# Two row tiles' attention logits on the two row halves of TensorE, with the keys held twice and W1 and W2 multiplied on chip

## The chip, the cores and the metric

The kernel runs on one core of a Trainium2 chip. A core has a matrix engine (TensorE, PE in the profile; its weight loads are listed apart as PEld), VectorE (DVE), ScalarE (ACT), GpSimd (POOL) and SyncE (SP, which here only issues transfers). Each engine works through its own instruction queue in order, and engines wait for each other through semaphores. TensorE writes its results to PSUM; ACT or DVE carry them on to SBUF. The metric is the device time of one execution in microseconds (us), the median over runs.

## The reference

A graph of 3327 nodes with 256 features goes through two layers; a dense weighted adjacency matrix `adj` is given. All values are float32. What matters for the change is the attention of layer 0, which is computed twice:

```
h  = relu(layernorm(x))                     # (3327, 256)
Xf = Xa = h
for n in range(2):
    q = Xa @ W1.T @ W2.T                    # (3327, 64)
    k = Xa @ W3.T                           # (3327, 64)
    probs = softmax(q @ k.T)                # (3327, 3327)
    A  = the largest probs of each row that reach 0.9 of its sum, renormalized
    Xf = R @ Xf                             # R: adj + identity, rows normalized
    Xa = A @ Xa
    Z  = Z + Xf @ U1[n].T + Xa @ U2[n].T
x = x + layernorm(h + Z) * ln_g + ln_b
```

Layer 1 is a graph attention with four heads over `adj > 0`; the change does not touch it.

## The kernel before

Rows are cut into 26 tiles of 128 (`NT`, the last one partly padding), and the tiles are worked on in 13 groups of two. A fast path (`fast`) runs first, and a slow general path only if a check at the end asks for it. In the profiled execution all the work shown is that of the fast path.

**Start.** The 26 tiles of x are loaded by SP's queue, DVE takes row statistics, DVE and ACT apply LayerNorm and relu (L553 to L555). Meanwhile ACT's queue issues the loads of W1, W3, W2, U1 and U2 (L545 to L549).

**Each of the two steps** has a prologue over all 26 tiles (L798 to L809). It transposes a tile on PE (`transposed`, L563, copied by ACT at L565), multiplies by W3 to get the transposed keys `kt`, 64 partitions by 3328 columns (L571, copied at L802), multiplies again to get the keys untransposed (L805, copied by ACT into `kk` at L808), and accumulates their second moments and their sum (L809), which go to `gm` (L810).

Then come the groups. `exponentials` takes the two tiles of a group one after the other. For each it makes the query in a chain of PE and ACT steps: transpose (L563, L565), times W1 (L571, L585), times W2 (L587, L589), and times `gm`, which yields the mean and the second moment of the row's logits (L591, copied at L593, finished by DVE at L594 and L595). Then it computes the tile's logits in seven chunks of 512 keys, each one matmul over 64 partitions (L604) into a PSUM buffer `pl`, from which ACT takes the exponential into `e` (L605), with row sums into `parts`. DVE adds the sums up (L608). A float32 matmul shows as two MATMUL records in the profile.

`top_p` finds each row's threshold on DVE. It begins with a Gaussian guess made of the mean and second moment: ACT needs its Ln table for L630 and its Exp table for L631, and again Ln at L633 and Exp at L645 and L648, each change of table being a load. It then evaluates masked sums over the 3327 exponentials (L660, two tiles per evaluation, four evaluations in step 0 and five in step 1), takes candidates (L703 to L728) and clears what falls below the threshold (L730).

`full_step` computes R @ Xf for a tile: SP loads the tile's columns of the transposed adjacency (L739), PE accumulates 26 matmuls (L741), DVE adds the tile itself (L743) and ACT divides (L746). `attention_step` computes A @ Xa: PE transposes `e` in blocks of four (L757) into a PSUM buffer `pt`, ACT copies them (L759), PE multiplies them (L766); each block's transposes are issued ahead of the previous block's matmuls. In step 1, `add_up` transposes the four results (L785, also into `pt`), multiplies by U1 and U2 into `z` (L791, a buffer of the pool `ps_m`), and DVE adds it to `main` (L792).

**Order.** The loop (L813 to L832) asks for the exponentials of the next group, then the full steps, `top_p` and attention of the present one. The program text does not fix the order on an engine: a planner orders each engine's instructions from the text, the dependences and the free buffers, so that L741 for instance is placed between the links of the query chain. The order is then fixed, and each queue works in it.

**Buffers.** PSUM tiles come from four pools of two buffers each: `ps_l` (logits, `pl`), `ps_acc` (accumulators), `ps_t` (`pt`) and `ps_m` (`pm`: all the small results of the chains, and `z`). `epool` holds four tiles of exponentials, two groups' worth.

Of the kernel before, what the change touches and what calls it, by code (L numbers as in the profile page):

```python
# [9 lines left out]
F32 = mybir.dt.float32  # L10
# [3 lines left out]
AF = mybir.ActivationFunctionType  # L14
ALU = mybir.AluOpType
# [453 lines left out]
def fast(  # L469
# [33 lines left out]
    def ln_stats(pool, t):  # L503
        st = pool.tile([P, V.BN_STATS_DIM], F32, name="bst")
        V.bn_stats(st, main[:, t, :D])
        V.bn_aggr(mv[:, t, :], st)
# [8 lines left out]
    with ExitStack() as l0:  # L515
        wpool = l0.enter_context(tc.tile_pool(name="wpool", bufs=1))
        w1 = wpool.tile([P, 2, DA], F32, name="w1")
        w3 = wpool.tile([P, 2, DA], F32, name="w3")
        w2 = wpool.tile([DA, DA], F32, name="w2")
        u1 = wpool.tile([P, STEPS, 2, D], F32, name="u1")  # L520
# [4 lines left out]
        xa1 = wpool.tile([P, NT, D + 1], F32, name="xa1")  # L525
        kt = wpool.tile([DA, NP], F32, name="kt")
        gm = wpool.tile([DA, 2 * DA + 1], F32, name="gm")
        V.tensor_copy(gm[:, :DA], ident[:DA, :DA])

# [7 lines left out]
        ps_acc = l0.enter_context(tc.tile_pool(name="ps_acc", bufs=2, space=PSUM))  # L537
        ps_t = l0.enter_context(tc.tile_pool(name="ps_t", bufs=2, space=PSUM))
        ps_m = l0.enter_context(tc.tile_pool(name="ps_m", bufs=2, space=PSUM))


        for t in range(NT):
            nc.sync.dma_start(main[:, t, :D], x[t * P : (t + 1) * P, :])
            ln_stats(small, t)
        nc.scalar.dma_start(w1, w1t.rearrange("(c p) o -> p c o", p=P))  # L545
        nc.scalar.dma_start(w3, w3t.rearrange("(c p) o -> p c o", p=P))
        nc.scalar.dma_start(w2, w2t)
        nc.scalar.dma_start(u1, u1t.rearrange("n (c p) o -> p n c o", p=P))
        nc.scalar.dma_start(u2, u2t.rearrange("n (c p) o -> p n c o", p=P))  # L549
# [18 lines left out]
        def projected(w, xt):  # L568
            ps = ps_m.tile([DA, P], F32, name="pm")
            for c in range(2):  # L570
                T.matmul(ps, w[:, c, :], xt[:, c, :], start=(c == 0), stop=(c == 1))  # L571
            return ps

        def exponentials(src, tiles):


            G = len(tiles)
            sm = small.tile([P, G], F32, name="sm")
            mu = small.tile([P, G], F32, name="mu")
            sq = small.tile([P, G], F32, name="sq")  # L580
            es = []
            for g, t in enumerate(tiles):
                ps = projected(w1, transposed(src, t))
                ut = small.tile([DA, P], F32, name="ut")
                S.copy(ut, ps)  # L585
                ps = ps_m.tile([DA, P], F32, name="pm")
                T.matmul(ps, w2, ut, start=True, stop=True)  # L587
                qt = small.tile([DA, P], F32, name="qt")
                S.copy(qt, ps)  # L589
                ps = ps_m.tile([P, 2 * DA + 1], F32, name="pm")  # L590
                T.matmul(ps, qt, gm, start=True, stop=True)  # L591
                qg = small.tile([P, 2 * DA + 1], F32, name="qg")
                S.copy(qg, ps)  # L593
                V.tensor_copy(mu[:, g : g + 1], qg[:, 2 * DA :])  # L594
                V.scalar_tensor_tensor(  # L595
                    qg[:, :DA], qg[:, :DA], 1.0, qg[:, DA : 2 * DA], ALU.mult, ALU.mult, accum_out=sq[:, g : g + 1]
                )
                e = epool.tile([P, NP], F32, name="e")
                nc.gpsimd.memset(e[:, N:], 0.0)
                parts = small.tile([P, NC], F32, name="parts")  # L600
                for c in range(NC):
                    w = min(512, N - 512 * c)
                    pl = ps_l.tile([P, 512], F32, name="pl")
                    T.matmul(pl[:, :w], qt, kt[:, 512 * c : 512 * c + w], start=True, stop=True)  # L604
                    S.activation(  # L605
                        e[:, 512 * c : 512 * c + w], pl[:, :w], AF.Exp, accum_out=parts[:, c : c + 1]
                    )
                V.tensor_reduce(sm[:, g : g + 1], parts, AX.X, ALU.add)  # L608
                es.append(e)
            return es, sm, mu, sq  # L610

# [183 lines left out]
        for n in range(STEPS):  # L795
            srcf, srca = (main, main) if n == 0 else (xf1, xa1)
            acc = ps_acc.tile([P, D + 1], F32, name="acc")
            for t in range(NT):  # L798
# [5 lines left out]
                for c in range(2):  # L804
                    T.matmul(ps, xt[:, c, :], w3[:, c, :], start=(c == 0), stop=(c == 1))  # L805
                kk = small.tile([P, DA + 1], F32, name="kk")
                nc.gpsimd.memset(kk[:, DA:], 1.0)
                S.copy(kk[:, :DA], ps)  # L808
                T.matmul(acc[:DA, : DA + 1], kk[:p, :DA], kk[:p, :], start=(t == 0), stop=(t == NT - 1))  # L809
            S.activation(gm[:, DA:], acc[:DA, : DA + 1], AF.Copy, scale=1.0 / N)  # L810
            groups = [list(range(t, min(t + 2, NT))) for t in range(0, NT, 2)]
# [240 lines left out]
```

## Time and profile before

| | |
|---|---|
| Median of 3 runs | 3086.12 us (3082.74 to 3088.73) |
| Profiled execution, its own time | 3073.39 us |
| Its span, first to last instruction | 3071.6 us |
| PE busy | 2756.5 us (90%) |
| DVE busy | 2387.5 us (78%) |
| ACT busy | 835.3 us (27%) |
| Mean granted PE clock | 0.923 |
| L604, logits on PE | 407.1 us in 728 records |
| L741, R @ Xf on PE | 336.4 + 335.8 us |
| L766, A @ Xa on PE | 322.8 + 323.3 us |

A group of lines names the line, engine and operation, what is written and read, how often, and the busy time. In a timeline, each row has the start, the length, the engine, the line, and in brackets how long the engine had sat idle before it and what ended that wait. Two clocks matter for PE: "PEclk" or "clock" is the share of its full speed that it was granted. A busy PE is not a PE at its peak, since matmuls are pipelined and their ends are modelled.

### The profile page before, as it was taken

Reading aid. Unit: us, or ns where it says so; the run is one execution under the profiler, and the core shown is the slowest. Engines: PE = TensorE matmul, PEld = TensorE weight load, DVE = VectorE, ACT = ScalarE, POOL = GpSimd, SP = SyncE. Lnnn points to the kernel's source line nnn. Section 1 sums busy time; section 2 is a strip of 40 time slices with the busy share of each in tenths; the row PEclk is TensorE's granted clock in tenths of the full one; section 3 lists DMA queues with packets and bytes.
Section 4 is the critical chain, followed back from the end, with each engine's and each line's share of the span. In section 5 each row is a group of like instructions: output and inputs, shape, how many; then the busy total and the mean of one; then the engine's idle time right before and its main releaser. Section 6 shows DMA issues by size and latency. Waiting matters only on the chain.

```text
span 3071.6 us, 32112 instructions
## 1 busy us (share of the span) xinstructions
PE 2756.5 (90%) x11078; PEld 1781.1 (58%) x11078; DVE 2387.5 (78%) x6069; ACT 835.3 (27%) x2036; POOL 54.5 (2%) x167
## 2 busy tenths in 40 slices
PE   6949999999999999389999999999995599999997
PEld 4427676666667685167777667666685433333334
DVE  3189887878788820899988888888893799999997
ACT  2423333333333324233233333333321300000000
POOL 0000000000000000000000000000001100000000
PEclk9759899999999999599999999999998799999998
DMA  3001111111111111001111111100121132222211
GB/s 108 23 0 45 45 45 45 45 45 45 45 45 45 45 56 34 0 11 41 49 48 47 48 47 49 49 31 33 38 71 37 52 104 83 82 77 71 89 55 33
DMA packets 77213, 150.69 MB, mean 49 GB/s; under 512 B 5489, under 2 KB 63600, under 8 KB 77040
## 3 DMA queue, kind: packets, MB, share of 16 engines
q1 hardware_dynamic: 74656, 146.56, 14.7%
q10 hardware_dynamic: 2384, 1.98, 0.2%
q8 instruction: 89, 1.46, 0.2%
q14 instruction: 84, 0.69, 0.1%
HBM read 145.11 MB, written 3.41 MB: 48 GB/s over the span
## 4 chain that ended last, share of the span: by engine, by line
PE 57%; DVE 33%; ACT 6%; issue 3%; DMA 1%; POOL 0%; ACTq 0%; DVEq 0%; POOLq 0%; SPq 0%
PE acc L950 19%; DVE y L660 18%; PE acc L741 13%; PE pl L604 11%; DVE cands L703 4%; PE acc L766 4%; PE pm L791 2%; PE pm L571 2%; ACT e L605 1%; PE pt L757 1%; ACT L630 1%; PE pm L805 1%; ACT L631 1%; PE pm L563 1%; DVE e L730 1%
## 5 line engine op out<-in xcount | busy, mean ns | idle before, releaser
L950 PE MATMUL acc<-e,hp 128*65 128x512 f32 (+1 forms) x1456 | 585.6, 562 | 1.8 <-DVE e L947 1.8
L947 DVE SCALAR_TENSOR_TENSOR e<-both,low,mask 128x512 f32<-128x512 f32 (+1 forms) x728 | 469.2, 708 | 38.4 <-PE acc L950 38.4
L660 DVE SCALAR_TENSOR_TENSOR y<-e,nt 128x3327 f32<-128x3327 f32 x130 | 478.8, 3683 | 2.3
L604 PE MATMUL pl<-kt,qt 64*128 64x512 f32 (+1 forms) x728 | 407.1, 698 | 54.8 <-ACT e L605 54.8
L950 PEld LDWEIGHTS acc<-e,hp 128*65 128x65 f32 x1456 | 198.1, 138 | 368.4 <-issue 255.3
L759 ACT COPY et<-pt 128x512 f32<-128x512 f32 (+1 forms) x364 | 199.4, 555 | 744.6 <-PE pt L757 744.6
L741 PE MATMUL acc<-main,at 128*128 128x257 f32 x1352 | 336.4, 402 | 0.1
L741 PE MATMUL acc<-xf,at 128*128 128x257 f32 x1352 | 335.8, 397 | 0.3 <-ACT xa L770 0.3
L766 PE MATMUL acc<-xa,et 128*128 128x257 f32 x1352 | 322.8, 382 | 3.8 <-ACT et L759 3.8
L766 PE MATMUL acc<-main,et 128*128 128x257 f32 x1352 | 323.3, 383 | 0.2
L604 PEld LDWEIGHTS pl<-kt,qt 64*128 64x128 f32 x728 | 144.2, 222 | 291.8 <-ACT e L605 229.4
L741 PEld LDWEIGHTS acc<-main,at 128*128 128x128 f32 x1352 | 262.6, 200 | 52.0 <-issue 13.3
L757 PE MATMUL pt<-ident,e 128*128 128x128 f32 x1352 | 202.1, 274 | 94.0 <-DVE e L730 94.0
L741 PEld LDWEIGHTS acc<-xf,at 128*128 128x128 f32 x1352 | 256.5, 197 | 49.4 <-issue 14.0
L766 PEld LDWEIGHTS acc<-xa,et 128*128 128x128 f32 x1352 | 245.4, 191 | 36.8 <-ACT et L759 7.6
L766 PEld LDWEIGHTS acc<-main,et 128*128 128x128 f32 x1352 | 245.0, 190 | 35.6 <-ACT et L759 6.2
L605 ACT ACTIVATE e<-pl 128x512 f32<-128x512 f32 (+1 forms) x364 | 205.2, 564 | 154.2 <-PE pl L604 151.2
L757 PEld LDWEIGHTS pt<-ident,e 128*128 128x128 f32 x1352 | 168.6, 141 | 127.7 <-DVE e L730 95.1
L703 DVE MAX8 cands<-y 128x8 f32<-128x208 f32 x832 | 237.2, 360 | 0.5
L660 DVE SCALAR_TENSOR_TENSOR y<-e,up 128x3327 f32<-128x3327 f32 x52 | 191.6, 3684 | 1.8
L730 DVE SCALAR_TENSOR_TENSOR e<-e,met 128x3327 f32<-128x3327 f32 x52 | 191.4, 3680 | 0.0
L660 DVE SCALAR_TENSOR_TENSOR y<-e,t 128x3327 f32<-128x3327 f32 x52 | 191.3, 3679 | 0.0
(183 smaller groups left out, 2091.9 us busy)
## 6 DMA issues: line engine op xcount, KB each, us to landing
at<-in_adjt_dram SPq DMA_DIRECT2D x104, 832.0 KB, 4.4
adjb<-in_adjt_dram SPq DMA_DIRECT2D x78, 512.0 KB, 3.6
main<-in_x_dram SPq DMA_DIRECT2D x26, 128.0 KB, 3.2
xh<-in_x_dram SPq DMA_DIRECT2D x26, 128.0 KB, 2.0
xr<-in_x_dram SPq DMA_DIRECT2D x26, 128.0 KB, 2.1
adjb<-in_adjt_dram SPq DMA_DIRECT2D x13, 256.0 KB, 2.7
out_dram<-r SPq DMA_DIRECT2D x25, 128.0 KB, 1.8
u<-in_u1t_dram ACTq DMA_DIRECT2D x1, 512.0 KB, 5.9
```

The lines of the kernel that those rows point to most:

```text
L571: T.matmul(ps, w[:, c, :], xt[:, c, :], start=(c == 0), stop=(c == 1))
L604: T.matmul(pl[:, :w], qt, kt[:, 512 * c : 512 * c + w], start=True, stop=True)
L605: S.activation(e[:, 512 * c : 512 * c + w], pl[:, :w], AF.Exp, accum_out=parts[:, c : c + 1])
L660: V.scalar_tensor_tensor(y, e[:, :N], th[:, k : k + 1], e[:, :N], ALU.is_lt, ALU.mult, accum_out=sums[:, k : k + 1])
L703: V.max(cands[:, k, c, :], y[:, c * PIECE : min(c * PIECE + PIECE, N)])
L730: V.scalar_tensor_tensor(e[:, :N], e[:, :N], nxt, e[:, :N], ALU.is_gt, ALU.mult)
L741: T.matmul(acc, at[:, j - j0, :], src[:, j, :], start=(j == 0), stop=(j == NT - 1))
L757: T.transpose(pt[:, k, :], e[:, (j0 + k) * P : (j0 + k + 1) * P], ident)
L759: S.copy(et[:, :n, :], pt[:, :n, :])
L766: T.matmul(acc, et[:, j - j0, :], src[:, j, :], start=(j == 0), stop=(j == NT - 1))
L947: V.scalar_tensor_tensor(e[:, k, :w], both[:, k, :w], low[:, j, k : k + 1], mask[:, j % JC, :w], ALU.max, ALU.mult)
L950: T.matmul(acc[k][:, :w], hp[:, j, k, :], e[:, k, :w], start=(j == 0), stop=(j == NT - 1))
```

## The change

The two tiles of a group now share one query tile `qt`: the first tile's transposed query lies in partitions 0 to 63, the second's in 64 to 127. The keys `kt` and the moments `gm` are held twice, in both halves. For that, W3 is held twice side by side, so that one 128-column multiplication writes both copies of the keys, and the query weights likewise. W1 and W2 are multiplied once at the start to `w12` (a transpose and a matmul for each half of W1's 256 rows), so the query chain loses one link.

`exponentials` first makes both queries and their moments, and then goes through the seven chunks, issuing for each chunk one matmul per tile, from partitions 0 to 63 and from 64 to 127, into the two banks of one `pl` buffer. ACT takes the two exponentials one after the other, and DVE adds up both tiles' sums in one instruction at the end. A `pl` buffer now takes two PSUM banks, and `ps_t` and `ps_m` have one buffer instead of two. In the prologue, ACT copies the untransposed keys twice into `kk`, and `gm` is written by two instructions.

```diff
-        w1 = wpool.tile([P, 2, DA], F32, name="w1")
-        w3 = wpool.tile([P, 2, DA], F32, name="w3")
-        w2 = wpool.tile([DA, DA], F32, name="w2")
+        w12 = wpool.tile([P, 2, 2, DA], F32, name="w12")
+        w3 = wpool.tile([P, 2, 2, DA], F32, name="w3")
...
-        kt = wpool.tile([DA, NP], F32, name="kt")
-        gm = wpool.tile([DA, 2 * DA + 1], F32, name="gm")
-        V.tensor_copy(gm[:, :DA], ident[:DA, :DA])
+        kt = wpool.tile([P, NP], F32, name="kt")
+        gm = wpool.tile([P, 2 * DA + 1], F32, name="gm")
+        for o in (0, DA):
+            V.tensor_copy(gm[o : o + DA, :DA], ident[o : o + DA, o : o + DA])
...
-        ps_t = l0.enter_context(tc.tile_pool(name="ps_t", bufs=2, space=PSUM))
-        ps_m = l0.enter_context(tc.tile_pool(name="ps_m", bufs=2, space=PSUM))
+        ps_t = l0.enter_context(tc.tile_pool(name="ps_t", bufs=1, space=PSUM))
+        ps_m = l0.enter_context(tc.tile_pool(name="ps_m", bufs=1, space=PSUM))
...
+        w1 = small.tile([P, 2, DA], F32, name="w1", bufs=1)
+        w2 = small.tile([DA, DA], F32, name="w2", bufs=1)
         nc.scalar.dma_start(w1, w1t.rearrange("(c p) o -> p c o", p=P))
-        nc.scalar.dma_start(w3, w3t.rearrange("(c p) o -> p c o", p=P))
         nc.scalar.dma_start(w2, w2t)
+        for r in range(2):
+            nc.scalar.dma_start(w3[:, :, r, :], w3t.rearrange("(c p) o -> p c o", p=P))
+        for c in range(2):
+            ps = ps_m.tile([DA, P], F32, name="pm")
+            T.transpose(ps, w1[:, c, :], ident)
+            w1r = small.tile([DA, P], F32, name="w1r")
+            S.copy(w1r, ps)
+            ps = ps_m.tile([P, DA], F32, name="pm")
+            T.matmul(ps, w1r, w2, start=True, stop=True)
+            for r in range(2):
+                S.copy(w12[:, c, r, :], ps)
...
         def projected(w, xt):
-            ps = ps_m.tile([DA, P], F32, name="pm")
+            ps = ps_m.tile([P, P], F32, name="pm")
             for c in range(2):
-                T.matmul(ps, w[:, c, :], xt[:, c, :], start=(c == 0), stop=(c == 1))
+                T.matmul(
+                    ps, w[:, c].rearrange("p r o -> p (r o)"), xt[:, c, :], start=(c == 0), stop=(c == 1)
+                )
...
+            qt = small.tile([P, P], F32, name="qt")
             es = []
             for g, t in enumerate(tiles):
-                ps = projected(w1, transposed(src, t))
-                ut = small.tile([DA, P], F32, name="ut")
-                S.copy(ut, ps)
-                ps = ps_m.tile([DA, P], F32, name="pm")
-                T.matmul(ps, w2, ut, start=True, stop=True)
-                qt = small.tile([DA, P], F32, name="qt")
-                S.copy(qt, ps)
+                half = slice(g * DA, g * DA + DA)
+                ps = projected(w12, transposed(src, t))
+                S.copy(qt[half], ps[half])
                 ps = ps_m.tile([P, 2 * DA + 1], F32, name="pm")
-                T.matmul(ps, qt, gm, start=True, stop=True)
+                T.matmul(ps, qt[half], gm[half], start=True, stop=True)
...
-                parts = small.tile([P, NC], F32, name="parts")
-                for c in range(NC):
-                    w = min(512, N - 512 * c)
-                    pl = ps_l.tile([P, 512], F32, name="pl")
-                    T.matmul(pl[:, :w], qt, kt[:, 512 * c : 512 * c + w], start=True, stop=True)
-                    S.activation(
-                        e[:, 512 * c : 512 * c + w], pl[:, :w], AF.Exp, accum_out=parts[:, c : c + 1]
-                    )
-                V.tensor_reduce(sm[:, g : g + 1], parts, AX.X, ALU.add)
                 es.append(e)
+            parts = small.tile([P, G, NC], F32, name="parts")
+            for c in range(NC):
+                lo, w = 512 * c, min(512, N - 512 * c)
+                pl = ps_l.tile([P, G, 512], F32, name="pl")
+                for g in range(G):
+                    half = slice(g * DA, g * DA + DA)
+                    T.matmul(pl[:, g, :w], qt[half], kt[half, lo : lo + w], start=True, stop=True)
+                for g, e in enumerate(es):
+                    S.activation(e[:, lo : lo + w], pl[:, g, :w], AF.Exp, accum_out=parts[:, g, c : c + 1])
+            V.tensor_reduce(sm, parts, AX.X, ALU.add)
...
-                    T.matmul(ps, xt[:, c, :], w3[:, c, :], start=(c == 0), stop=(c == 1))
-                kk = small.tile([P, DA + 1], F32, name="kk")
-                nc.gpsimd.memset(kk[:, DA:], 1.0)
-                S.copy(kk[:, :DA], ps)
-                T.matmul(acc[:DA, : DA + 1], kk[:p, :DA], kk[:p, :], start=(t == 0), stop=(t == NT - 1))
-            S.activation(gm[:, DA:], acc[:DA, : DA + 1], AF.Copy, scale=1.0 / N)
+                    T.matmul(ps, xt[:, c, :], w3[:, c, 0, :], start=(c == 0), stop=(c == 1))
+                kk = small.tile([P, 2 * DA + 1], F32, name="kk")
+                nc.gpsimd.memset(kk[:, 2 * DA :], 1.0)
+                for r in range(2):
+                    S.copy(kk[:, r * DA : r * DA + DA], ps)
+                T.matmul(acc[:, : DA + 1], kk[:p, : 2 * DA], kk[:p, DA:], start=(t == 0), stop=(t == NT - 1))
+            for o in (0, DA):
+                S.activation(gm[o : o + DA, DA:], acc[o : o + DA, : DA + 1], AF.Copy, scale=1.0 / N)
```

## The prediction

> **What bounds the kernel now.** I read the page's summary first, then busy time by window, then the timeline of one group of two row tiles, PE, ACT and DVE together.
>
> ```profile
> PE 2756.5 (90%) x11078; PEld 1781.1 (58%) x11078; DVE 2387.5 (78%) x6069; ACT 835.3 (27%) x2036; POOL 54.5 (2%) x167
> ...
> PEclk9759899999999999599999999999998799999998
> ```
>
> The averages only say that PE leads and DVE follows. PE's clock is low at the start of each attention step. By window (busy us and instructions of PE, PEld, DVE, ACT, POOL, then clock, DMA share, GB/s):
>
> ```profile
> 110.00:200.00 90.00, 63.66 (x115) 26.57 (x114) 45.65 (x146) 38.87 (x101) 0.00 (x0) 0.50 0.00 0
> ...
> 200.00:397.00 197.00, 171.48 (x753) 130.33 (x754) 180.84 (x473) 56.01 (x131) 0.59 (x6) 0.89 0.11 35
> ...
> 700.99:776.35 75.36, 71.56 (x305) 52.07 (x305) 60.94 (x168) 26.22 (x62) 0.20 (x2) 0.93 0.14 46
> ...
> 1865.88:1951.25 85.37, 80.65 (x357) 59.61 (x357) 72.80 (x197) 29.05 (x67) 0.20 (x2) 0.96 0.13 44
> ```
>
> There are three regimes. At a step's start two groups of logits run at clock 0.50. Then DVE binds for about three groups (180.84 of 197), because full_step matmuls were already done in the prologue. From about the fourth group on PE binds: one group takes some 76 us in step 0 and 85.4 in step 1, with PE nearly full and DVE at 61 and 73. In the list of the longest pieces of the critical chain, L703 starts at 248.91 and 311.02, 62 us apart: the DVE-bound period of step 0. In step 1 it starts at 1286.48 and, three groups on, at 1508.67: 74 us. So a PE saving counts down to 62 and 74, not below.
>
> Inside a group, the logits of the second tile (start, length, engine, line, what, count, wait):
>
> ```profile
> 700.83 6.35 PE L604 MATMUL pl<-kt,qt 64*128 64x512 f32 x14
> ...
> 712.70 1.28 ACT L630 ACT_TABLE_LOAD   x1
> ...
> 714.21 1.28 ACT L631 ACT_TABLE_LOAD   x1
> ...
> 715.62 0.58 ACT L605 ACTIVATE e<-pl 128x512 f32<-128x512 f32 x1
> ...
> 716.18 0.59 ACT L605 ACTIVATE e<-pl 128x512 f32<-128x512 f32 x1
> ...
> 716.34 6.33 PE L604 MATMUL pl<-kt,qt 64*128 64x512 f32 x8 [2.48 <-ACT e L605]
> ...
> 722.60 21.57 PE L741 MATMUL acc<-main,at 128*128 128x257 f32 x92
> ...
> 723.22 0.16 DVE L608 TENSOR_REDUCE sm<-parts 128x1 f32<-128x7 f32 x1 [11.08 <-ACT e L605]
> ```
>
> The first tile takes 6.3 us for seven chunks of two instructions. In the second, the Ln and Exp table loads hold ACT's in-order queue, PE fills its two pl buffers, idles 2.48 us and comes back at half speed: weight loads 0.85 us apart instead of 0.43. So 14 instructions need 6.28 us in one tile and 11.73 us (710.87 to 722.60) in the other. About 1.8 us more of slow clock falls in the first L741 matmuls (92 in 21.57, against 0.215 each at full speed). DVE idles 11.08 us for these logits. ACT alone does a chunk in 0.56 us (715.62 to 716.18, both inputs ready).
>
> **What the Trainium skill says.** "TensorE: Matmul & The Clock Gate", Part 3 (The mechanism): matmuls at different row groups overlap, while starts and ends stay in program order. Before uses only rows 0 to 63, so no trace of it shows this. Its Part 1 puts an idle array at half clock and restores it after some 3.4 us of activity. The trace agrees on the half, but at 138.72 us fourteen 64-row matmuls take 11.29 us and stay at half. "TensorEngine Tiling (Array Packing)", Gotcha 1: row tiles must write different PSUM banks. The pl tile does, at two banks per buffer. "PSUM — Partial Sum Buffer", "The four PSUM rules": eight banks. Before uses 2+2+2+2, after 4+2+1+1, which is why ps_t and ps_m fall to one buffer.
>
> **The change part by part**, per group unless said otherwise.
>
> *Removed, L585/L587.* One matmul pair (0.43 us of PE) and its ACT copy. The link is 1.0 us long (709.03 to 710.02) but hidden by 0.70 us of L741. I take 0.43 x 2 = 0.9 us (0.9 to 2).
>
> *Logits as pairs of half arrays.* Same instruction count. Unknown: does fp32, which runs here as two instructions per product, overlap between halves? Bounds: a pair costs 0.86 us if yes, 1.71 if no, and 1.71 or 3.42 at half clock. I take yes. Unwaited ACT then needs 1.12 a pair. var (L628) now exists before the logits begin, so I place the two table loads after the first exponential or two, as before after the second tile's first chunk. PE then has done pairs 0 and 1 by 2.15 us, and ACT is free again near 4.7. Pair 0's second exponential frees its buffer near 5.4. PE has idled about 3 us and I take half clock again: 4.5 pairs x 1.71 = 7.7, end 13.1, with 0.5 us of latency 13.6. Before: 6.28 + 11.73 = 18.0. Gain 4.4. If the clock stays full, 9 + 3 = 12 and no residue of 1.8: gain 7.8. With 0.9 for L587: 5.3 a group, up to 8.7.
>
> *Order.* Both query chains now come before all logits. Their waits were covered by L741 (eight instructions at 707.27 to 710.87) and still can be; uncovered, the second chain costs 2.8 us.
>
> *ps_t 2 to 1.* An attention tile starts with two transpose blocks back to back:
>
> ```profile
> 1905.94 1.04 PE L757 MATMUL pt<-ident,e 128*128 128x128 f32 x8
> ...
> 1906.57 1.07 ACT L759 COPY et<-pt 128x512 f32<-128x512 f32 x2 [7.66 <-PE pt L757]
> ...
> 1907.21 2.01 PE L766 MATMUL acc<-xa,et 128*128 128x257 f32 x8 [0.24 <-ACT et L759]
> ```
>
> The second block must now wait for the first copy: 0.5 + 0.8 + 0.5 = 1.85 us instead of 1.28, so 0.55 us a tile. Later blocks are covered: a copy is over (1910.32) 0.7 us before the next transposes (1911.02). I take 0.8 a group (0 to 1.1). In step 1 add_up's second L785 also shares the buffer: 0.5 more.
>
> *ps_m 2 to 1.* z of add_up (L789) holds the only buffer until DVE's L792, and the next group's L563 waits for it:
>
> ```profile
> 1947.38 0.38 PE L563 MATMUL pm<-ident,xa 128*128 128x128 f32 x2
> ...
> 1947.80 0.40 DVE L792 SCALAR_TENSOR_TENSOR main<-xh,pm 128x256 f32<-128x256 f32 x1
> ```
>
> That is 1 us, or up to 3.7 if L792 stands behind one L660 pass. Behind L563 on PE stand the query chain and the logits. Step 1 penalty in all: 2.3 (0.8 + 0.5 + 1). In the prologue L805 must wait for the kt copy: L563's successor comes 0.65 us later per tile, 34 us over both steps uncovered. L741 can cover it as it covers the other waits there (six instructions in each 3.2 us tile). I take 10.
>
> *Rest.* The second kk copy (0.21 us on ACT) is in those 0.65. 128-column weight loads in L571: L805 already issues 128-column loads at 0.13 us each, no slower than L571's 0.15, so nothing. W1 x W2 and the second w3 DMA fall under the x loads and LayerNorm (first matmul at 24.31 us, ACT idle until 21.23); uncovered about 6 us, two 2 to 3 us landings. One L608 in place of two and two gm writes: under 0.3 us.
>
> *Step start.* Group 0's sm comes at 134.90, 26.7 us after its first logit at 108.24. After: 108.24 - 1.0 + 2.8 + 13.6 + 0.9 = 124.5, 10 us earlier, and DVE, which binds next, starts 10 us earlier. Twice: 20.
>
> **Sum.** PE-bound groups: ten a step (logits 3 to 12). Step 0: 10 x (5.3 - 0.8) = 45. Step 1: 10 x (5.3 - 2.3) = 30. Starts 20, prologues -10. Net 85 us off the profiled execution's 3073.4 (span 3071.6), 2988. The runs shown have their median 12.7 us above it, so 3001: I say 3000. Periods become 71.5 and 82.4, still above the DVE floors of 62 and 74.
>
> **Rivals.**
> 1. *More than this.* The paired halves keep or regain full clock: 10 x 7.9 + 10 x 6.4 + 10 + 10 = 163 to 173 less, about 2920. If L741 is also placed into the logits' waits, the DVE floor ends it: 10 x 14 + 10 x 11 less, about 2850. For: full-array L741 does recover the clock. Against: before never has L741 between logits.
> 2. *The halves do not overlap* (the change doesn't do what it says), and this ends slower. A pair is 3.42 us once the clock is half, and the stall now falls at the head of both tiles, not of one: 5.4 + 4.5 x 3.42 = 20.8 against 18.0. Less 0.9, plus 0.8 and 2.3: 2.7 and 4.2 a group, 69 over twenty, plus 10 for prologues: about 3160. For: no trace shows fp32 overlap. Against: halves use separate rows and banks. It decides from about 2.6 us a pair at half clock.
> 3. *The single buffers eat the gain.* Attention starts 29 us, prologues 34, and L792 twice behind an L660 pass in ten groups, 74: 137 against a gross gain of 126, about 3095. For: DVE is in order and 3.7 us passes are its bulk. Against: the waits in before are filled.
>
> **How the numbers follow.** Main case 0.50 (its own range 2955 to 3040), rival 1 0.18 (2850 to 2955), rival 2 0.20 (3100 to 3190), rival 3 0.12 (3040 to 3115). About 0.08 of rival 1 lies below 2900 and 0.10 of rival 2 above 3150: range 2900 to 3150. A change within 0.2% (6 us) can't be told from none. Faster: 0.50 + 0.18 + 0.02 of rival 3 = 0.70. Same: 0.04. Slower: 0.20 + 0.06 = 0.26.
>
> **What would show it.** Right: pairs of the new L604 0.86 us apart at full clock or 1.71 at half, ACT's exponentials two close together, one PE idle of about 3 us per group near the head of the logits, group periods near 71 and 82, first sm of a step 10 us earlier. Wrong: pairs at 3.42 (rival 2); clock at 1.0 through the logits or L741 among them (rival 1); PE waiting on L792 or on L759 for more than 2 us a group (rival 3); or L630 waiting in ACT's queue for a mu that DVE has not yet made.

## The result, and the profile after

The changed kernel takes 11800.47 us (median of four runs, 11791.0 to 11803.16) against 3084.43 us (3080.19 to 3088.73) for the kernel before, run beside it: a ratio of 3.8252, with a 95% interval of 3.8186 to 3.8319. The forecast of 3000 us, with a range of 2900 to 3150, is wrong by a factor of almost four, and no case that it weighed comes near.

The profile of the changed kernel, its summary and one row of its slices:

```profile
span 11800.7 us, 65994 instructions
...
PE 5473.1 (46%) x21848; PEld 3558.9 (30%) x21848; DVE 10757.8 (91%) x14142; ACT 2380.0 (20%) x4448; POOL 108.8 (1%) x278
...
PEclk7999899999766666666665666666666666658998
```

PE issues 21848 matmul records where it had issued 11078, DVE works 10757.8 us where it had worked 2387.5, and the span has twice the instructions. A change of PE's order or of PSUM buffers can't do that: work has been added. The costliest groups of the page, by line, say which:

```profile
L196 DVE SCALAR_TENSOR_TENSOR scr<-e,cand 128x3327 bf16<-128x3327 f32 x1404 | 5124.4, 3684 | 35.6 <-ACT e L177 12.7
...
L676 DVE SCALAR_TENSOR_TENSOR y<-e,nt 128x3327 f32<-128x3327 f32 x130 | 478.8, 3683 | 2.3
```

L676 is the masked sum of the fast path (L660 before). L196 stands in `general`, the path that runs only if the verdict at the end of `fast` asks for it: 1404 passes are 27 for each of 26 tiles in each of two steps. The timelines show where it begins. The kernel before ends its fast path with the verdict, and little follows:

```profile
3063.68 0.14 DVE L1005 TENSOR_SCALAR redo<-bad 1x1 int32<-1x1 f32 x1
```

In the changed kernel (the same statement is L1023):

```profile
3040.27 0.15 DVE L1022 TENSOR_TENSOR bad<-verdict 1x1 f32<-1x1 f32 x1
3040.45 0.14 DVE L1023 TENSOR_SCALAR redo<-bad 1x1 int32<-1x1 f32 x1
3041.32 0.84 SPq L123 DMA_DIRECT2D main<-in_x_dram  x2
```

The verdict comes 23.2 us earlier than before. Then x is loaded anew (L123), and the whole network is computed a second time, from 3041 to 11800 us. So there are two questions: why the verdict changed, and why the fast path gained 23 us where 85 were forecast.

**Where the fast path's 23 us come from.** Marks in both timelines: the start of the last write of `gm` in each step (L810, now L828), of the copy of a group's sums into `met` (L624, now L640), and of `redo`. A negative difference is a gain.

| Stretch | before, us | after, us | difference | forecast |
|---|---|---|---|---|
| start and prologue of step 0, to `gm` | 106.2 | 140.0 | +33.8 | +10 for both prologues |
| to the third group's sums | 160.0 | 146.2 | -13.9 | -10 |
| ten group periods, to the last sums of step 0 | 760.7 | 704.7 | -56.0 | -45 |
| end of step 0 and prologue of step 1, to `gm` | 174.6 | 207.9 | +33.3 | (above) |
| to the third group's sums | 181.6 | 169.0 | -12.6 | -10 |
| ten group periods, to the last sums of step 1 | 845.2 | 831.6 | -13.6 | -30 |
| the rest, to `redo` | 835.4 | 841.2 | +5.8 | 0 |
| sum, to `redo` | 3063.7 | 3040.5 | -23.2 | -85 |

**The logits.** One group of the changed kernel, step 0, on PE:

```profile
690.10 1.88 PE L622 MATMUL pl<-kt,qt 64*128 64x512 f32 x4
...
692.98 1.99 PE L622 MATMUL pl<-kt,qt 64*128 64x512 f32 x8
695.47 1.13 PE L622 MATMUL pl<-kt,qt 64*128 64x512 f32 x4 [0.51 <-ACT e L624]
699.65 2.93 PE L622 MATMUL pl<-kt,qt 64*128 64x512 f32 x8 [3.06 <-ACT e L624]
```

The eight records at 692.98 are two pairs of logits, four float32 products of 64 by 512, in 1.99 us. Within a pair the two products start 7 ns apart: the halves overlap, as forecast. The four records at 690.10 are only two products, one after the other, and they take nearly as long, 1.88 us. The planner had put the first tile's first two products (685.90 and 687.65) ahead of the second tile's query, so that in this group, as in most later ones, five of the seven pairs run side by side and two do not. The forecast had all seven side by side. PE then idles 3.06 us for ACT, as forecast. The same group on ACT:

```profile
694.74 0.59 ACT L624 ACTIVATE e<-pl 128x512 f32<-128x512 f32 x1
...
695.44 1.28 ACT L646 ACT_TABLE_LOAD   x1
...
696.95 1.28 ACT L647 ACT_TABLE_LOAD   x1
...
698.36 0.58 ACT L624 ACTIVATE e<-pl 128x512 f32<-128x512 f32 x1
```

The two table loads come after the third pair, not after the first exponential or two, so only the last two pairs follow PE's pause. They take 2.93 us, although the last chunk has only 255 columns. The same group on DVE:

```profile
691.13 3.68 DVE L746 SCALAR_TENSOR_TENSOR e<-e,met 128x3327 f32<-128x3327 f32 x1
694.73 0.15 DVE L642 TENSOR_TENSOR var<-mu 128x2 f32<-128x2 f32 x1
...
703.81 0.17 DVE L625 TENSOR_REDUCE sm<-parts 128x2 f32<-128x14 f32 x1 [8.52 <-ACT e L624]
...
705.32 0.16 DVE L650 TENSOR_TENSOR u<-u,mu 128x2 f32<-128x2 f32 x1 [0.95 <-ACT u L649]
```

DVE finishes the group before (L746), makes `var`, and has nothing to do until the sums: 8.52 us, plus 0.95 for the Ln of the guess. In the kernel before, a group had 11.08 for the sums (the line of L608 in the prediction), and:

```profile
711.37 0.15 DVE L594 COPY mu<-qg 128x1 f32<-128x1 f32 x1 [0.72 <-ACT qg L593]
...
724.73 0.16 DVE L634 TENSOR_TENSOR u<-u,mu 128x2 f32<-128x2 f32 x1 [0.96 <-ACT u L633]
```

That is 3.3 us less in a group, and the period fell by 3.5, from 75.4 to 71.9.

**The prologue.** The window of step 0's prologue (PE, PEld, DVE, ACT and POOL busy, clock, DMA share, GB/s), before and then after:

```profile
24.00:106.20 82.20, 74.86 (x419) 51.83 (x420) 9.62 (x31) 30.69 (x107) 2.46 (x25) 1.00 0.13 44
```

```profile
24.00:139.80 115.80, 89.67 (x418) 68.37 (x418) 10.26 (x33) 34.11 (x133) 2.46 (x26) 0.77 0.10 32
1124.00:1198.80 74.80, 57.61 (x255) 43.55 (x254) 0.59 (x2) 17.15 (x72) 1.57 (x16) 0.66 0.08 26
```

The same 418 or 419 matmul records take 33.6 us more. PE is idle for 26.1 us of them instead of 7.3, and busy for 14.8 us longer, since the clock falls from 1.00 to 0.77. The last row is the latter part of step 1's prologue, at 0.66. The planner fills waits of the prologue with matmuls of the full steps (L757); they are its cover. The last of them starts at 82.9 us. From there to the prologue's end the clock is 0.54, and a tile looks like this on PE:

```profile
93.20 1.12 PE L821 MATMUL pm<-w,xt 128*128 128x64 f32 x4 [0.35 <-ACT kt L818]
94.91 0.66 PE L826 MATMUL acc<-kk 128*128 128x65 f32 x2 [0.58 <-ACT kk L825]
95.36 0.63 PE L577 MATMUL pm<-ident,main 128*128 128x128 f32 x2
96.51 1.22 PE L586 MATMUL pm<-xt,w 128*128 128x128 f32 x4 [0.52 <-ACT xt L579]
98.09 1.12 PE L821 MATMUL pm<-w,xt 128*128 128x64 f32 x4 [0.35 <-ACT kt L818]
```

With one `pm` buffer each of a tile's three small results waits for ACT's copy of the one before it, and each piece runs at half clock. A tile takes 4.89 us (93.20 to 98.09). In the kernel before, the cover ends too, at 92.0 us, but with two `pm` buffers a tile then takes 1.98 us, at a clock of 1.00:

```profile
93.98 0.30 PE L809 MATMUL acc<-kk 128*64 128x65 f32 x2 [0.24 <-ACT kk L808]
94.25 0.65 PE L571 MATMUL pm<-xt,w 128*64 128x128 f32 x4
94.83 0.66 PE L805 MATMUL pm<-w,xt 128*128 128x64 f32 x4
95.33 0.39 PE L563 MATMUL pm<-ident,main 128*128 128x128 f32 x2
95.96 0.30 PE L809 MATMUL acc<-kk 128*64 128x65 f32 x2 [0.25 <-ACT kk L808]
```

With the cover between the links a tile takes 3.54 us, against 3.18 before.

### The profile page after: what moved, and what is told of

Its sections match the earlier page's. It is cut to its first block, busy times and chain, and to the rows that moved or that the text cites. A ratio compares the mean times of both kernels' runs of the same rounds, so it can differ in the third digit from the quotient of the medians.

```text
span 11800.7 us, 65994 instructions
## 1 busy us (share of the span) xinstructions
PE 5473.1 (46%) x21848; PEld 3558.9 (30%) x21848; DVE 10757.8 (91%) x14142; ACT 2380.0 (20%) x4448; POOL 108.8 (1%) x278
## 4 chain that ended last, share of the span: by engine, by line
DVE 73%; PE 19%; ACT 4%; issue 3%; DMA 1%; another core or an unknown queue 0%; POOL 0%; SPq 0%; ACTq 0%; POOLq 0%; DVEq 0%
DVE scr L196 38%; DVE y L676 6%; PE acc L968 5%; DVE e L435 3%; DVE junk L385 3%; DVE scr L214 3%; DVE e L443 3%; PE acc L255 2%; PE pl L171 2%; DVE scr L218 2%; DVE e L210 2%; DVE e L219 2%; PE acc L757 1%; PE acc L782 1%; DVE e L439 1%
## 5 line engine op out<-in xcount | busy, mean ns | idle before, releaser
L196 DVE SCALAR_TENSOR_TENSOR scr<-e,cand 128x3327 bf16<-128x3327 f32 x1404 | 5124.4, 3684 | 35.6 <-ACT e L177 12.7
L444 PE MATMUL acc<-e,hp 128*65 128x512 f32 (+1 forms) x1456 | 717.9, 641 | 347.7 <-DVE e L443 347.7
L968 PE MATMUL acc<-e,hp 128*65 128x512 f32 (+1 forms) x1456 | 585.6, 562 | 2.0 <-DVE e L965 2.0
L676 DVE SCALAR_TENSOR_TENSOR y<-e,nt 128x3327 f32<-128x3327 f32 x130 | 478.8, 3683 | 2.3
L435 DVE SCALAR_TENSOR_TENSOR e<-both,sd,e 128x512 f32<-128x512 f32 (+1 forms) x728 | 471.5, 707 | 8.9 <-ACT e L434 8.9
L434 ACT ACTIVATE e<-both,dlow 128x512 f32<-128x512 f32 (+1 forms) x728 | 443.8, 678 | 51.9 <-PE acc L444 51.9
L443 DVE SCALAR_TENSOR_TENSOR e<-adjb,e 128x512 f32<-128x512 f32 (+1 forms) x728 | 427.3, 646 | 4.6 <-ACT e L440 4.4
L440 ACT ACTIVATE e<-e 128x2048 f32<-128x2048 f32 (+1 forms) x182 | 325.4, 1788 | 245.9 <-DVE e L439 245.7
L385 DVE CUSTOM_DVE_ANT_0 junk<-an,db 128x3327 bf16<-128x3327 f32 (+1 forms) x104 | 370.7, 3624 | 2.0 <-ACT db L370 1.2
L214 DVE TENSOR_TENSOR_SCAN scr<-scr 128x3327 uint16<-128x3327 bf16 x52 | 368.5, 7086 | 0.0
L255 PE MATMUL acc<-main,et 128*128 128x257 f32 x1352 | 353.2, 409 | 0.0
L255 PE MATMUL acc<-xa,et 128*128 128x257 f32 x1352 | 343.2, 400 | 3.8 <-ACT et L248 3.8
L782 PE MATMUL acc<-xa,et 128*128 128x257 f32 x1352 | 328.5, 388 | 0.0
L782 PE MATMUL acc<-main,et 128*128 128x257 f32 x1352 | 321.8, 382 | 0.0
L757 PE MATMUL acc<-main,at 128*128 128x257 f32 x1352 | 320.2, 392 | 0.0
```

Of the source, the lines that this page charges most:

```text
L196: V.scalar_tensor_tensor(junk, e[:, :N], cand[:, g : g + 1], e[:, :N], ALU.is_ge, ALU.mult, accum_out=sums[:, g : g + 1],)
L214: V.tensor_tensor_scan(rank, ties, ties, 0.0, ALU.add, ALU.max)
L255: T.matmul(acc, et[:, j - j0, :], src[:, j, :], start=(j == 0), stop=(j == NT - 1))
L385: V.tensor_tensor_reduce(junk[:p], an[:p], db[:p, k, :N], scale=1.0, scalar=-BIG, op0=ALU.add, op1=ALU.max, accum_out=top[:p, t, k : k + 1],)
L435: V.scalar_tensor_tensor(e[:, k, :w], both[:, 0, k, :w], sd[:, j, 1, k : k + 1], e[:, k, :w], ALU.add, ALU.max)
L443: V.scalar_tensor_tensor(ek, adjb[:, :n, j % JC, :], 0.0, ek, ALU.is_gt, ALU.mult)
```

## The experiments

The theory for the second run of the network: the verdict asks for it because W1 x W2 multiplied first rounds the queries differently, which makes one row's threshold fall between two equal exponentials. The test is L1000: the number of exponentials kept, `met[:, 2]`, must equal the number strictly above the largest one dropped, `met[:, 4]`. The rivals: another condition of the verdict, or a fault of the half arrays or of the doubled keys. Ratios below are to the kernel before, run beside each experiment (about 3078 us each time).

### e1_chain: the queries through W1 and W2 again, all else of the change kept

```diff
...
-                ps = projected(w12, transposed(src, t))
+                xt = transposed(src, t)
+                ps = ps_m.tile([DA, P], F32, name="pm")
+                for c in range(2):
+                    T.matmul(ps, w1[:, c, :], xt[:, c, :], start=(c == 0), stop=(c == 1))
+                ut = small.tile([DA, P], F32, name="ut")
+                S.copy(ut, ps)
+                ps = ps_m.tile([P, P], F32, name="pm")
+                T.matmul(ps, w2.rearrange("p r o -> p (r o)"), ut, start=True, stop=True)   # w2 held twice
...
```

> The changed kernel with one part undone: queries again by W1 and then W2 (W2 held twice side by side), keys and moments still held twice, logits still side by side, one buffer each in ps_t and ps_m. Theory R (rounding): the product W1 x W2 rounds the queries otherwise, and with these numbers one row's smallest kept exponential equals a dropped one exactly, so the verdict orders the general path; with the old rounding it does not, and the time is that of the fast path, about 3063 us plus or minus 12 (the changed kernel's fast path ends 23 us earlier than before's; the chain gets its link back). Theory H (halves): something that the half arrays or the doubled keys and moments deliver trips the verdict; then the general path still runs and the time is about 11800 us.

3117.96 us, a ratio of 1.0137 (1.0103 to 1.0172), and no second run. With the old rounding and the new halves the verdict is content. It is some 55 us slower than expected; the time is taken up under e12.

### e2_w12_only: the kernel before, with W1 x W2 alone

```diff
...
-                ps = projected(w1, transposed(src, t))
-                ut = small.tile([DA, P], F32, name="ut")
-                S.copy(ut, ps)
-                ps = ps_m.tile([DA, P], F32, name="pm")
-                T.matmul(ps, w2, ut, start=True, stop=True)
+                ps = projected(w12, transposed(src, t))
```

> The kernel before with one part of the change alone: W1 and W2 multiplied once on chip, everything else as before (one tile after the other, keys held once, two buffers in all pools). Theory R: the rounding is that of the changed kernel, the general path runs, about 3080 + 8760 = 11830 us. Theory H: no general path, about 3060 to 3085 us.

11804.58 us in its one run. Its page has the second path's group again, with neither halves nor doubled keys in the kernel:

```profile
L196 DVE SCALAR_TENSOR_TENSOR scr<-e,cand 128x3327 bf16<-128x3327 f32 x1404 | 5124.2, 3683 | 32.1 <-ACT e L177 9.3
```

So the product W1 x W2 is enough for it, and the halves are not needed.

### e3_no_tie_test and e4_tie_but_one_tile: the changed kernel, the tie condition left out

```diff
         V.tensor_tensor(one, met[:, 2], met[:, 4], ALU.not_equal)
+        V.memset(one[:, 47:48], 0.0)       # e4 only: tile 21 of step 1
         V.tensor_add(bad, bad, one)        # e3: this line and the first taken out
```

> The changed kernel with one of the verdict's five conditions left out, the one that compares the number of kept exponentials with the number of those strictly above the largest dropped one (met rows 2 and 4, a tie at the cut). Theory R: no general path, about 3061 us (23 below before), plus or minus 5. Theory H, through the window's count, a full piece of candidates, the range of the sum or the logits' reach: still about 11800 us.

> The changed kernel with the tie condition kept for all row tiles of both steps except tile 21 of step 1 (column 47 of met), where it is left out. Theory R in its sharpest form, one row in that one tile: no general path, about 3061 us. If ties are spread over several tiles, or lie in another: about 11800 us.

e3: 3050.43 us, 0.9909 (0.9873 to 0.9946). e4: 3054.1 us in one run. The tie condition alone asks for the second run, and of the 52 tiles of both steps only tile 21 of step 1 raises it. A float32 calculation of the attention off the chip, which had named this tile, finds it in one row: its smallest kept exponential and its largest dropped one are the same number. The row itself is shown by no run.

### e5_after_swapped_order and e6_before_swapped_order: only the order of a sum changed

```diff
-        def projected(w, xt):
+        def projected(w, xt, order=(0, 1)):
...
-            for c in range(2):
-                T.matmul(..., start=(c == 0), stop=(c == 1))
+            for c in order:
+                T.matmul(..., start=(c == order[0]), stop=(c == order[1]))
...
-                ps = projected(w12, transposed(src, t))
+                ps = projected(w12, transposed(src, t), (1, 0))     # e6: w1
```

The query's two halves of 128 features are added up in the other order. e5 does it in the changed kernel, e6 in the kernel before; the verdict is whole in both.

> The changed kernel, whole, with its verdict whole, and one difference that costs nothing: the query's matmul adds up its two halves of 128 features in the other order (second half first), which only rounds the queries otherwise. Theory R: the tie is an accident of rounding and a float32 calculation of this order has none, so no general path: about 3050 us, as in the run without the tie test, plus or minus 8. A rival, that the product W1 x W2 or the half arrays make values that tie or go wrong whatever the order: about 11800 us.

> The kernel before, with nothing of the change, and the same swap of order in its query matmul (W1, second half of the features first). Theory R: rounding alone decides; a float32 calculation of this order has one tie, in tile 13 of step 1, so the general path runs, about 3085 + 8760 = 11845 us. Rival, that before's structure is safe from ties: about 3080 us.

e5: 3047.24 us, 0.9894 (0.9853 to 0.9935). e6: 11817.42 us in one run; the page of e6 has:

```profile
L196 DVE SCALAR_TENSOR_TENSOR scr<-e,cand 128x3327 bf16<-128x3327 f32 x1404 | 5124.3, 3684 | 35.6 <-ACT e L177 12.7
```

This settles it: the same mathematics and the same instructions, added in another order, and the changed kernel is 1.1% faster than before, or the kernel before takes 11817 us. The calculation off the chip puts e6's tie in another tile, 13 of step 1. Of four roundings of the queries (two orders, with and without the product), two ask for the second run. e5 is therefore no safer than the rest; it has a rounding without a tie for these inputs. From here on e5 is the changed kernel with its fast path alone, and the next experiments are built on it.

### e9_one_half: both queries in partitions 0 to 63

```diff
-            qt = small.tile([P, P], F32, name="qt")
+            qts = [small.tile([DA, P], F32, name="qt%d" % g) for g in range(G)]
...
-                    half = slice(g * DA, g * DA + DA)
+                    half = slice(0, DA)
+                    qt = qts[g]
```

> As the changed kernel with swapped order (3047 us), but both tiles' queries lie in partitions 0 to 63, so both logits of a pair use the same half of the array; everything else, the order of issue too, is kept. Theory O (the halves overlap, and that is what the groups won): pairs 1.71 us apart at full clock and 3.42 at half instead of 0.86 and 1.71, 6 to 8 us more a group in some twenty groups and 10 more for each of the four groups at the steps' starts: 3190 to 3250 us. Rival (the groups won by the missing link and the early table loads, the overlap is hidden behind ACT and DVE): 3045 to 3070 us.

3154.77 us, 1.0259 (1.0223 to 1.0294): 107 us above e5. The logits of one of its groups:

```profile
648.26 5.41 PE L624 MATMUL pl<-kt,qt 64*128 64x512 f32 x12
655.78 5.48 PE L624 MATMUL pl<-kt,qt 64*128 64x512 f32 x8 [2.11 <-ACT e L626]
```

Twelve records, three pairs, take 5.41 us, and after PE's pause the last two pairs take 5.48, where the changed kernel needs 1.99 for two pairs and 2.93 for the last two. The overlap of the halves is real for float32 and is worth more than the whole gain: without it the same program is slower than before. Its late group periods are 75.1 us in step 0 and 85 to 89 in step 1, against 71.9 and 82 to 85 in e5.

### e7_prologue_in_logit_banks: the prologue's keys in the logits' buffers

```diff
-                ps = projected(w3, xt)
+                pl = ps_l.tile([P, 2, 512], F32, name="pl")
+                ps = projected(w3, xt, ps=pl[:, 0, :P])
...
-                ps = ps_m.tile([P, DA], F32, name="pm")
+                ps = pl[:, 1, :DA]
```

> As the changed kernel with swapped order, but the two prologues take the PSUM tiles of their key projections from the logits' buffers, which are idle then, instead of from the single ps_m buffer. Theory P (the single ps_m buffer costs what the prologues lost): step 0's prologue ends at about 110 us instead of 139.8, step 1's gains some 15, the whole is about 3005 us (45 below the swapped order). Rival (the prologues' loss is hidden or is due to the wider weight loads and the second kk copy): 3045 to 3050 us.

2930.95 us, 0.9514 (0.9475 to 0.9553): 116 us below e5, and 74 below what was expected. `ps_l` is idle in the prologue; with the two key products there, only the transpose is left in `ps_m`. The prologue's window and two tiles of it on PE:

```profile
24.00:89.50 65.50, 57.09 (x369) 50.44 (x370) 8.60 (x27) 33.56 (x133) 2.48 (x25) 1.00 0.05 17
```

```profile
50.07 0.41 PE L827 MATMUL acc<-kk 128*128 128x65 f32 x2
50.31 0.39 PE L577 MATMUL pm<-ident,main 128*128 128x128 f32 x2
50.53 0.60 PE L757 MATMUL acc<-main,at 128*128 128x257 f32 x2
50.97 0.55 PE L822 MATMUL pl<-w,xt 128*128 128x64 f32 x4
51.36 0.66 PE L586 MATMUL pl<-xt,w 128*128 128x128 f32 x4
52.11 0.41 PE L827 MATMUL acc<-kk 128*128 128x65 f32 x2
```

No wait is left on PE, the clock is 1.00, and a tile takes 2.04 us (50.07 to 52.11). The time to `gm` falls from 139.3 us in e5 to 89.7, and the stretch with step 1's prologue from 207.9 to 156.6; 13 us more come from the two starts, and the group periods hardly move. Not all of it is the chain: e7's first prologue takes in only 51 records of L757 (16.2 us) where the changed kernel's takes in 104 (31.1 us), so some 15 us of matmuls move on to the start of step 0. That start is shorter all the same, so they must lie in pauses of PE there.

### e8_three_single_banks, e10_two_transpose_buffers and e11_both: the eight banks dealt out anew

```diff
-        ps_l = l0.enter_context(tc.tile_pool(name="ps_l", bufs=2, space=PSUM))
+        ps_l = l0.enter_context(tc.tile_pool(name="ps_l", bufs=3, space=PSUM))
-        ps_t = ... bufs=1        # e10: 2
-        ps_m = ... bufs=1        # e8, e11: 2
...
-                pl = ps_l.tile([P, G, 512], F32, name="pl")
+                pls = [ps_l.tile([P, 512], F32, name="pl") for _ in range(G)]
```

Logits take three single banks instead of two pairs, and the bank that this frees goes to `ps_m` or to `ps_t`. e10 and e11 also have e7's prologue.

> As the changed kernel with swapped order, but the PSUM banks dealt out otherwise: each half's logits in a bank of its own, three such buffers (3 banks instead of 4), so ps_m gets two buffers back (2), ps_t stays at one, ps_acc at two. Theory P: prologues as in before (step 0's ends near 108 us), and the query chains wait less: about 3000 us. Rival, that three logits buffers slow the pairs (a half must wait for ACT before the next pair): each group loses 1 to 3 us, about 3030 to 3060.

> As the run with three single banks and two ps_m buffers (2958 us), and in addition the prologues' key projections in the logits' banks. If the prologues still waited for ps_m there: 2925 to 2940 us, below the run with the prologue alone only if the second ps_m buffer helps the query chains too (then about 2910). If two ps_m buffers were already enough for the prologues: 2955 us.

> As the run with the prologue in the logits' banks (2931 us), but each half's logits in a bank of its own, three such buffers, so that ps_t gets its second buffer back (ps_l 3, ps_acc 2, ps_t 2, ps_m 1). Theory T (the single ps_t costs the waits seen at the start of each attention tile, 0.46 and 2.2 us in a group of step 0, and as much or more in step 1): 2.5 to 3.5 us less a group, about 2865 us. Rival (three logits buffers instead of four banks cost as much as that): 2920 to 2950 us.

e8: 2958.08 us, 0.9607 (0.9568 to 0.9645). e11: 2909.33 us, 0.9455 (0.942 to 0.949). e10: 2889.4 us, 0.9381 (0.9343 to 0.9419). The last is the best version, 6.2% faster than the kernel before, with the verdict whole. Part of a group of e10 on PE:

```profile
567.01 4.07 PE L622 MATMUL pl<-kt,qt 64*128 64x512 f32 x8 [2.50 <-ACT e L624]
571.01 24.36 PE L757 MATMUL acc<-main,at 128*128 128x257 f32 x98
595.21 1.03 PE L773 MATMUL pt<-ident,e 128*128 128x128 f32 x8
```

The attention's two transpose blocks stand back to back again (eight records at 595.21). The three single banks do change the logits: ACT frees one bank at a time, the two products of a pair start 0.58 us apart instead of together, and the last two pairs take 4.07 us against 2.93. All the same, from its first product to its last a group's logits take 16.1 us (554.95 to 571.08), against 16.7 in the changed kernel (685.90 to 702.58). The next part of the same story is on DVE, the end of one group and the wait for the next:

```profile
632.35 3.68 DVE L746 SCALAR_TENSOR_TENSOR e<-e,met 128x3327 f32<-128x3327 f32 x1
643.30 0.17 DVE L625 TENSOR_REDUCE sm<-parts 128x2 f32<-128x14 f32 x1 [6.99 <-ACT e L624]
```

The late periods, read from the sums' copies, are 71.7 us in step 0, nearly the 71.9 of the changed kernel, and 79.6 to 80.7 in step 1 against 82.4 to 85.0. (e11, with one `pt` buffer and two `pm`: 71.1 to 73.0, and 81.2 to 84.0.) So in step 0 neither a second `pt` nor a second `pm` shortens the period. By the trace DVE sets it, with its own passes, its wait for the sums, and in e10 1.26 us for L757 beside the 6.99; no run takes these waits away. In step 1 the bank gives about 2 us a group more as a second `pt` (e10) than as a second `pm` (e11).

### e12_w12_only_swapped: the kernel before with W1 x W2, in the order without a tie

The edit is that of e2 and that of e5 together.

> The kernel before with W1 and W2 multiplied once on chip as its only structural change, and the swapped order in the query's matmul, for which a float32 calculation finds no tie. The prediction's working (0.9 us a group, the link being hidden by L741): about 18 us less than before, 3060. Rival, read from the 70 us between the changed kernel with and without the chain (3118 and 3047): the link is on the path even with two ps_m buffers, 3010 to 3030 us.

3054.77 us, 0.9931 (0.9902 to 0.9959): the link is worth 24 us in the old layout by the medians, 13 to 30 by the interval. The profiled execution is one of its two slowest of six (3067.3 us): its span is only 6.2 us shorter than that of before, and the late periods stay at 75.1 to 75.4 and 85.3. The profile of e2 shows more. Its fast path is the same program but for the order of the sum, and it ends 16.5 us earlier than that of before: 9.4 of them come in ten periods of step 0 and 13.7 in those of step 1, where a late group takes 83.8 to 84.3 us instead of 85.4 (other stretches give back the rest). Why one program has 85.3 in one execution and 83.8 in the other is open. In the new layout the link is dearer: e1 is 71 us above e5. By the same marks, 18 us of that lie in ten periods of step 0 (72.8 to 74.4 us each against 71.9), 29 in those of step 1, and 18 in the two starts. That the link holds the only `pm` buffer, which the other chain then waits for, would explain it; no run doubles that buffer with the link kept, so this is argued, not shown.

## Why the prediction was wrong

**The step that failed.** It is the sentence of the sum on W1 x W2, "fall under the x loads and LayerNorm", and the removal of L585/L587 at 0.9 us a group: the working took this part of the change for a matter of time only, and every case, the rivals too, ran the fast path alone. But (x W1) W2 and x (W1 W2) are the same only in exact arithmetic. The kernel has a test on equality of two counts, and a branch on it that costs 8760 us (3040.5 to 11800.7). e2 shows that this part alone is enough, e3 and e4 that it is the tie in one tile, e6 that the kernel before falls into it when two products are added in the other order. The profile could not have told that a tie would come, but the code told that it could: a branch taken on data, and an edit that changes the data's last bits. That was a rival to be named. Its price could be estimated from the profile before: a second computation, called slow, takes at least as long as the fast one, some 3060 us. What chance to give it, nothing then at hand could say. That the kernel before escapes the branch is the luck of its rounding, and e5's order was taken because the calculation off the chip found no tie for it.

**The fast path, by the steps of the sum** (3047.24 us in e5 against the forecast of 3000, which lies in rival 3's range, 3040 to 3115, and not in the main case's, 2955 to 3040):

- *Halves overlap*: right, for five of the seven pairs. The profile after has them 0.96 us apart at full clock (692.98 to 693.94), PE's long pause of 3.06 us, and e9 prices the overlap at 107 us. That the planner would run the first tile's first two products ahead was not foreseen. The Trainium skill, "TensorE: Matmul & The Clock Gate", Part 3 (The mechanism), says that matmuls of different row groups overlap; here they do so for float32 products of two instructions each, two pairs in 1.99 us against three pairs in 5.41 without overlap (e9).
- *Half clock for 4.5 pairs after the pause*: wrong. It was 1.5 pairs (the last chunk is half as wide) in 2.93 us, since the table loads stand after the third pair.
- *Step starts*: right in kind, 13.9 and 12.6 us against 10.
- *PE-bound periods down to 71.5 and 82.4*: the times came out at 71.9 and 83.6, but the reason given for step 0 probably did not. Its period follows DVE's waits (12.8 us a group before, 9.5 after), and giving `ps_t` its second buffer back left it at 71.7. In the profile after, the chain of work that ended last is in step 0, from 418 to 991 us, 49% DVE's passes L676 and L719, and 8% PE's L757 and L782. This is read from traces, not shown by a run. Forecast -45 and -30 for the two steps, measured -56.0 and -13.6.
- *ps_t, 0.8 us a group*: mis-sized on PE and misplaced in effect. In the late groups of step 0 the second tile's transposes waited 2.0 to 2.7 us for ACT's copy, because ACT stood in its queue at L786, waiting for DVE's L785 behind a 3.7 us pass:

```profile
668.30 0.60 PE L773 MATMUL pt<-ident,e 128*128 128x128 f32 x4
...
671.71 0.65 PE L773 MATMUL pt<-ident,e 128*128 128x128 f32 x4 [2.37 <-ACT et L775]
```

  In step 0 it cost the period nothing that e10 shows; in step 1 about 2 us a group (e10 against e11).
- *Prologues, 10 of 34 us*: the largest error of the sum, 57 us too low. Measured +33.8 and +33.3. The working had the link (L805 behind the copy of `kt`), and took L741 for the cover as far as it was needed. But 104 records at six a tile last for 17 of the 26 tiles, and a tile without cover grew by 2.9 us (1.98 to 4.89), not by 0.65: it has three waits, not one, and the pieces between them run at half clock, 1.6 to 1.9 times as long (0.63 against 0.39 us for a transpose, 1.22 against 0.66 for the product with W3). e7, which changes only these buffers, has neither wait nor slow clock: 1.00 and 65.5 us in place of 0.77 and 115.8.
- *The rest*: 5.8 us later from the last sums of step 1 to `redo`, which was not looked for, and whose cause is open. The sum of these errors, 57 for prologues, 16 for step 1 and 6 here, less 11 for step 0 and 6 for the starts, is the 62 us between -85 and -23. Two small sums do not come out as written, and change nothing here: 0.5 + 0.8 + 0.5 is 1.8, not 1.85, and 250 us off 3086 are 2836, not 2850.

**The rivals.** Rival 2's price of about 3160 us for halves that do not overlap meets e9's 3155, but by accident: it had 69 us in the groups and 10 in the prologues, and e9 has two thirds of a hundred in the prologues and about none in the twenty periods together (19 less in step 0, 21 more in step 1). Rival 3, that the single buffers eat the gain, named the right thing with the wrong weights: it gave the prologues 34 us, where the runs show 67, and L792 behind DVE's passes 74, where the profile after shows no wait of PE for it.

## What to carry to other kernels

Before any edit that changes how a sum is rounded, look for a branch or a test that depends on the computed values: a mathematically equal form can switch a fallback on, and its price is then the fallback's, not the edit's. Where a pool falls from two buffers to one, walk through every stretch that uses it, also those in which its cover runs out, and count the clock that the engine loses to the pauses. When banks are short, ask which pool lies idle in that stretch: here the logits' banks, idle in the prologue, turned a gain of 1% into one of 5%, and dealing the banks out again into 6%.

## What the runs showed of the hardware

- Two float32 products of 64 rows by 512 columns, on rows 0 to 63 and 64 to 127, take together about what one takes alone: in the changed kernel four products in two pairs took 1.99 us, and two that followed one another 1.88. With both on the same half (e9) the kernel is 107 us slower.
- Three pauses of 0.35 to 0.58 us between small matmuls, in each tile of 4.89 us, went with a clock of 0.54 from 82.9 to 139.8 us: a transpose of two records takes 0.63 us there and 0.39 where no pause is left (e7). One pause of 0.25 us in each tile of 1.98 us, in the kernel before from 92 to 106 us, left the clock at 1.00.
- The order in which two matmuls add into one accumulator changes the result in bits that a test on equality sees: e5 and e6 differ from their parents in nothing else.
